# Layer 1 attention with a context: projections of the next two heads in three pieces, and three PSUM banks for transposes in that stage

## The chip, the cores and the metric

The kernel runs on one core of one Trainium2 chip, as one program. The metric is the device time of one execution in microseconds (us); the median of several runs stands for a version. A core has a matrix engine (TensorE, PE in the profile; its weight loads are listed as PEld), a vector engine (VectorE, DVE), a scalar engine (ScalarE, ACT), GpSimd (POOL) and SyncE (SP, which here issues DMAs). Each engine runs its own instructions in order and waits for others through semaphores. PE writes its results to PSUM, which this program uses as banks of 128 partitions by 512 float32; DVE and ACT carry ("evacuate") them from there to SBUF, from where PE takes its operands.

## The reference

A post-norm decoder of two layers over 8 batches of 512 tokens of width 256, with a context of 64 tokens for each batch, all in float32. Six steps follow one another, each with a residual and a layer norm:

```
x = LN(x + L0_attn(x))          # 16 heads of 16, scores times a decay of the distance
x = LN(x + L0_xattn(x, ctx))    # attention to the context
x = LN(x + L0_ffn(x))           # butterfly maps around a GELU
x = LN(x + L1_attn(x))          # 16 heads of 64, rotary, causal
x = LN(x + L1_xattn(x, ctx))    # the stage that is changed most
x = LN(x + L1_ffn(x))           # 8 experts, the best 2 for each token
```

What matters here is the fifth:

```
def _L1_xattn_ref(x1, x2, Wq1, Wk1, Wv1, Wk2, Wv2, Wo, bo):   # 8 heads of 64
    q1, k1, v1 = heads(x1 @ Wq1), heads(x1 @ Wk1), heads(x1 @ Wv1)
    k2, v2 = heads(x2 @ Wk2), heads(x2 @ Wv2)
    k, v = concat(k1, k2), concat(v1, v2)                     # 512 + 64 keys
    attn = softmax(q1 @ k.T * 64 ** -0.5)
    return (attn @ v) @ Wo + bo
```

The sixth, the experts, begins with a routing: a norm, a transposition, a product with the router's weights, the best two of eight, and for each token its rank in its expert's list, by which its row is scattered to memory.

## The kernel before, in words

Time order is batch by batch inside a stage, and stage by stage. In the profiled execution the stages lie about so: layer 0 self-attention 0 to 830 us, layer 0 context attention and feed-forward to 1262, layer 1 self-attention to 2234, layer 1 context attention to some 3130, the experts to 3660, and the last norm.

**PSUM.** Three pools are open at a time: `s` (tiles of two banks, for scores and wide products), `t` (one bank, tiles for transposes) and `o` (one bank, for outputs that are accumulated). Layer 0 self-attention has 3, 1 and 1 such tiles; everything after it 2, 2 and 2, which is eight banks. A pool gives its buffers in turn, and a tile waits until the buffer's earlier tile has been read. `evac` (L96 to L104) carries a bank to SBUF, on DVE and ACT in turns: L102 is DVE's copy, L104 ACT's.

**Layer 1 with the context** is a software pipeline (`_pipeline`, L32). Its units are (batch b, pair of heads c, block of 128 queries i), 8 by 4 by 4 = 128. In step n each stage runs on unit n minus its lag, in the order of the list; after the stages, one piece of postponed work (`put_off`) runs. The PE's order is exactly this program order (`manual_schedule`), while a scheduler places the instructions of DVE and ACT. The stages:

- `l1x_pre`, lag 0, works only at i = 0. At c = 0 it transposes the batch's x (`x_transposed`, L192) and makes the context's values (L1008) for this batch in 64 partitions, `vx`. Then for the pair of heads it makes q and k (L1020) in one `s` tile, evacuated by ACT (L1022, q) and DVE (L1023, k), and v (L1027) in a `t` tile, evacuated by ACT (L1035).
- `l1x_scores`, lag 1: for each of two heads j the scores with 512 keys (L1047) and with 64 context keys (L1048) in one `s` tile; DVE takes the maximum (L1049), ACT the exponential with its sum (L1050), and `scaled` (L883 to L885) divides on DVE.
- `l1x_transposes`, lag 3: eight 128x128 transposes (L287) in two `t` tiles named tP, each evacuated by `evac`.
- `l1x_values`, lag 7: the product with v (L1081), accumulated in an `o` tile over the four key blocks; at the fourth also the context's values (L1088), and `out_done` starts the output projection (L233, by postponed pieces).
- `l1x_last_transposes`, lag 3, stands last in the list: the transposes of the 64 context columns of both heads (L1069) in a third `t` tile tP2 of that step.

The postponed work of a finished batch is, a piece for every second step: the output projection in two pieces (L233), then `route_norm`, `route_transposes` (tiles tZ, L1146, evacuated by ACT to `xnT`, L1147), `route_picks` (tile o_r, L1161) and `route_places` (tile o_rank, L1200 to L1204; then on POOL the scatters L1216). `xnT` shares the tag "xT", which has two buffers, with the transposed x of `x_transposed`.

**Layer 0 self-attention** (L580 to L612) runs over 32 units of (batch, four heads). A unit has four steps kt. Each makes scores for the softmax (`l0_probs`), values (`l0_values`) and the maxima two units ahead (`l0_maxima`, L419); at kt = 3 a piece from the list `later` follows (the transposes and the output of a finished batch, whose norm ends with ACT's L215 on x, or the preparation of the next one). After the four steps comes `l0_project`, the q and k of three units ahead (L402, L403, evacuated by ACT at L404 and L405). Here a scheduler places PE's instructions too; around these lines the order it gives is the program's.

**Experts.** A pipeline over blocks of 256 or 128 token rows: load, transposes (tZ, L1351), up (s_h, L1373), down (o_y, L1390), and a scattered addition on POOL (L1411). The first block's rows are read back from `rows_in`, after the scatters.

Of the kernel before, what the change touches and what calls it, by code (L numbers as in the profile page):

```python
# [18 lines left out]
P = 128  # L19
# [30 lines left out]
def decoder_kernel(ctx: ExitStack, tc: tile.TileContext, a: dict, out: bass.AP):  # L50
# [19 lines left out]
    @contextmanager  # L70
    def psum(name, s, t, o):

        with (
            tc.tile_pool(name=f"ps_s{name}", bufs=s, space=PSUM) as pp["s"],
            tc.tile_pool(name=f"ps_t{name}", bufs=t, space=PSUM) as pp["t"],
            tc.tile_pool(name=f"ps_o{name}", bufs=o, space=PSUM) as pp["o"],
        ):
            yield

    def phase(name):  # L80
# [3 lines left out]
    def slot(name):  # L84
        return ring.tile([P, SLOT], F32, tag="slot", name=name)
# [6 lines left out]

    def o_tile(name):
        return pp["o"].tile([P, 512], F32, tag="o", name=name)

    n_evac = [0]  # L96

    def evac(dst, src):

        n_evac[0] += 1  # L100
        if n_evac[0] % 2:
            dve.tensor_copy(dst, src)  # L102
        else:
            act.copy(dst, src)  # L104
# [119 lines left out]
    def project_and_norm(b, lhs, w, n, plus, later=None):  # L224

        r = r_tile()

        def piece(i2):
            o = o_tile("o_out").rearrange("p (i n) -> p i n", i=2)
            for j in range(2):  # L230
                i = 2 * i2 + j
                for c in range(n):
                    pe.matmul(  # L233
                        o[:, j, :],
                        lhsT=lhs[:, c, i * P : (i + 1) * P],
                        rhs=w[:, c, :],
                        start=(c == 0),
                        stop=(c == n - 1),
                    )
# [303 lines left out]
    with tc.tile_pool(name="bfly", bufs=1, side="right") as bfly, phase("l0_self") as ph, psum("a", 3, 1, 1):  # L543
# [76 lines left out]
    ctx.enter_context(psum("b", 2, 2, 2))  # L620


    wqT = slot("wqT").rearrange("p (c n) -> p c n", c=KC)
# [347 lines left out]
        )  # L971


    q1_k1 = slot("q1_k1")
    v1_k2 = slot("v1_k2")
    v2_o = slot("v2_o")
# [10 lines left out]

    pts = [[slot("pt").rearrange("p (k n) -> p k n", k=NT) for _ in range(2)] for _ in range(2)]
    for c in range(4):
        o = o_tile("o_k2")  # L990
# [10 lines left out]
    def l1x_pre(b, c, i):  # L1001
        if i:
            return
        if c == 0:
            xT = x_transposed(b)
            o = o_tile("o_v2")
            for kc in range(KC):
                pe.matmul(  # L1008
                    o[0:S2, :], lhsT=ctxT[:, kc, b * S2 : (b + 1) * S2], rhs=wv2[:, kc, :], start=(kc == 0), stop=(kc == KC - 1)
                )  # L1010
            vx = work.tile([P, S], F32, tag="lat", name="vx")
            evac(vx[0:S2, :], o[0:S2, :])
            live["xT", b], live["vx", b] = xT, vx
        xT = live["xT", b]
        cols = slice(c * P, (c + 1) * P)
        q, k = qk_tiles()
        s = s_tile("s_qk")
        for j, w in enumerate((wq1, wk1)):
            for kc in range(KC):
                pe.matmul(s[:, j, :], lhsT=w[:, kc, cols], rhs=xT[:, kc, :], start=(kc == 0), stop=(kc == KC - 1))  # L1020

        act.mul(q, s[:, 0, :], 0.125)  # L1022
        dve.tensor_copy(k, s[:, 1, :])  # L1023
        t = t_tile("t_v")
        for j in range(NT):
            for kc in range(KC):
                pe.matmul(  # L1027
                    t[:, j, :],
                    lhsT=xT[:, kc, j * P : (j + 1) * P],
                    rhs=wv1[:, kc, cols],  # L1030
                    start=(kc == 0),
                    stop=(kc == KC - 1),
                )
        v = ph.tile([P, NT, P], F32, tag="vc", name="vc", bufs=3)
        act.copy(v, t)  # L1035
        live["qkv", b, c] = q, k, v

    def l1x_scores(b, c, i):
        q, k, _ = live["qkv", b, c]
        p = p_tile(S + S2, bufs=4)  # L1040
        sums = col("sums", 4)
        nm = col("nm", 2)
        for j in range(2):
            h = 64 * j
            lhsT = q[h : h + 64, i * P : (i + 1) * P]
            s = s_tile("s_sc").rearrange("p t n -> p (t n)")
            pe.matmul(s[:, 0:S], lhsT=lhsT, rhs=k[h : h + 64, :], start=True, stop=True)  # L1047
            pe.matmul(s[:, S : S + S2], lhsT=lhsT, rhs=k2[h : h + 64, c, b * S2 : (b + 1) * S2], start=True, stop=True)  # L1048
            dve.tensor_reduce(nm[:, j : j + 1], s[:, 0 : S + S2], AX.X, ALU.max, negate=True)  # L1049
            act.activation(  # L1050
                p[:, j, :], s[:, 0 : S + S2], AF.Exp, bias=nm[:, j : j + 1], accum_out=sums[:, j : j + 1]
            )
        scaled(p, sums, S + S2)
        live["p", b, c, i] = p

    def l1x_transposes(b, c, i):
        p = live["p", b, c, i]
        if i == 0:
            live["pt", b, c] = pts[c % 2], ph.tile([P, 2, S], F32, tag="pt2", name="pt2")
        pt, _ = live["pt", b, c]  # L1060
        probs_transposed(p, [pt[j][:, :, i * P : (i + 1) * P] for j in range(2)], NT)

    def l1x_last_transposes(b, c, i):

        p = live.pop(("p", b, c, i))
        _, pt2 = live["pt", b, c]
        t = t_tile("tP2")
        for j in range(2):
            pe.transpose(t[0:S2, j, :], p[:, j, S : S + S2], ident)  # L1069
        evac(pt2[0:S2, :, i * P : (i + 1) * P], t[0:S2, 0:2, :])  # L1070

    def l1x_values(b, c, k):

# [11 lines left out]
            return  # L1085
        for j in range(2):
            h = c * P + 64 * j
            pe.matmul(o[64 * j : 64 * (j + 1)], lhsT=vx[0:S2, h : h + 64], rhs=pt2[0:S2, j, :], start=False, stop=True)  # L1088

        def plus():  # L1090
            xb = work.tile([P, NT, D], F32, tag="att", name="xb")
# [63 lines left out]

    def route_picks(b):
        xnT = live.pop(("xnT", b))
        o = o_tile("o_r")[:, 0 : NT * NE].rearrange("p (i e) -> p i e", e=NE)
        for i in range(NT):
            for c in range(KC):  # L1160
                pe.matmul(  # L1161
# [33 lines left out]
    def route_places(b):  # L1195

        picks, both = live.pop(("picks", b))
        o = o_tile("o_rank")
# [184 lines left out]
    def moe_down(n):  # L1383
        _, mine, size = where[n]
        h = live.pop(("h", n))
        xr, _, w2, cells = live.pop(("load", n))
        o = o_tile("o_y").rearrange("p (i n) -> p i n", i=TILES)
        for i in range(size):
            for f in range(8):
                pe.matmul(  # L1390
# [159 lines left out]
```

## Time and profile before

| | us |
|---|---|
| three runs | 3712.23, 3716.97, 3719.49 |
| median | 3716.97 |
| the profiled execution | 3704.71 |
| its span, first to last instruction | 3703.0 |
| PE busy in the span | 3483.6 (94%) |
| DVE busy | 2190.3 (59%) |
| ACT busy | 1447.7 (39%) |
| POOL busy | 1091.5 (29%) |

The profile is one execution. A group of the profile is a source line, an engine, and what it writes and reads; its busy time is the sum over its instructions, and "idle before" is time in which the engine stood still just ahead of an instruction of that group, with the event that ended the wait. The timeline gives neighbouring instructions of one group as one row with a count. A float32 product appears as several records for one call: `x8` for q and k is two products in two parts each, and two records for every part. "PEclk" and the clock of a window are the share of the full TensorE clock that was granted.

### The profile page before, as it was taken

The page shows a single profiled execution, that of the slowest core. Times are in us where ns is not written, and L with a number is a line of the kernel's source. Part 1 is how long each engine was busy: PE and PEld are TensorE (multiplying, and loading weights), DVE is VectorE, ACT ScalarE, POOL GpSimd, SP SyncE. Part 2 cuts the span into 40 slices and gives each one's busy share as a digit, 9 for nine tenths or more (in the row PEclk, how much of TensorE's full clock was granted, in tenths as well). Part 3 has the DMA queues.
Part 4 walks back from the last instruction along what each step waited for, and adds up shares of the span by engine and source line. Part 5 has one row for each costly group of instructions (what it writes and reads, how often), then busy time and mean ns, then how long its engine had stood idle before and what let it go on. Part 6 is the DMA issues. An engine that isn't in the chain of part 4 may idle for free. (4 is left out here: it accounts for less than half of the span.)

```text
span 3703.0 us, 53042 instructions
## 1 busy us (share of the span) xinstructions
PE 3483.6 (94%) x19862; PEld 2149.2 (58%) x19862; DVE 2190.3 (59%) x6160; ACT 1447.7 (39%) x2949; POOL 1091.5 (29%) x960
## 2 busy tenths in 40 slices
PE   8999899988999899999999999999999998999995
PEld 3344334446666556665666665555555555888884
DVE  5766777647666377778777775665666655110102
ACT  2444444443333244445444443433334333222222
POOL 3877787751211122222222210010101101222222
PEclk8999999987999999999999999999999999999997
DMA  4100011120000395233222320000000001766674
GB/s 130 30 24 24 24 37 36 35 59 9 4 1 1 84 277 120 35 41 40 37 35 35 41 41 1 6 13 18 18 11 14 18 12 58 241 188 180 185 232 136
DMA packets 165363, 233.94 MB, mean 63 GB/s; under 512 B 26441, under 2 KB 128521, under 8 KB 165106
## 3 DMA queue, kind: packets, MB, share of 16 engines
q1 hardware_dynamic: 138370, 174.78, 15.1%
q0 software_dynamic: 25584, 51.57, 9.4%
q10 hardware_dynamic: 1152, 4.19, 0.3%
q8 instruction: 157, 2.57, 0.3%
q14 instruction: 100, 0.82, 0.1%
HBM read 135.83 MB, written 61.11 MB: 53 GB/s over the span
## 5 line engine op out<-in xcount | busy, mean ns | idle before, releaser
L424 DVE CUSTOM_DVE_ANT_0 scored<-s_sc,decay 128x512 f32<-128x512 f32 x512 | 323.2, 687 | 231.1 <-PE s_sc L419 229.9
L853 POOL DMA_DIRECT2D qk<-turned x256 | 202.8, 1206 | 668.8 <-PE t_v L860 284.1
L477 ACT ACTIVATE pt<-s_st 128x1024 f32<-128x1024 f32 x256 | 261.3, 1024 | 263.0 <-PE s_st L473 232.0
L277 ACT ACTIVATE p<-p,nm 128x128 f32<-128x128 f32 (+3 forms) x512 | 283.1, 554 | 160.4 <-DVE nm L275 157.5
L104 ACT COPY pt<-tP 128x512 f32<-128x512 f32 (+2 forms) x416 | 212.5, 511 | 298.3 <-PE tP L931 196.9
L1050 ACT ACTIVATE p<-s_sc,nm 128x576 f32<-128x576 f32 x256 | 189.7, 743 | 294.6 <-DVE nm L1049 256.5
L885 DVE TENSOR_SCALAR p<-p,rsum 128x576 f32<-128x576 f32 (+4 forms) x768 | 296.2, 427 | 5.5
L1410 DVE TENSOR_SCALAR y<-o_y,share 128x256 f32<-128x256 f32 x71 | 31.4, 480 | 403.6 <-PE o_y L1390 403.6
L1373 PE MATMUL s_h<-xnT,we 128*128 128x256 f32 (+1 forms) x1248 | 262.4, 364 | 1.9 <-DMA we<-in_mo_w 1.9
L102 DVE COPY pt<-tP 128x512 f32<-128x512 f32 (+2 forms) x416 | 248.3, 597 | 14.8 <-PE tP L1069 6.8
L1390 PE MATMUL o_y<-we,h 128*128 128x256 f32 x1136 | 251.6, 379 | 0.0
L265 DVE CUSTOM_DVE_ANT_0 p<-s_sc,tabs 128x128 f32<-128x128 f32 (+3 forms) x512 | 233.0, 484 | 20.7 <-PE s_sc L899 20.7
L1373 PEld LDWEIGHTS s_h<-xnT,we 128*128 128x128 f32 x1248 | 218.1, 193 | 27.1 <-DMA we<-in_mo_w 2.3
L1390 PEld LDWEIGHTS o_y<-we,h 128*128 128x128 f32 x1136 | 215.2, 190 | 28.9
L1411 POOL DMA_INDIRECT total<-y,to x71 | 110.1, 1551 | 397.3 <-DVE y L1410 206.0
L899 PE MATMUL s_sc<-qk 64*128 64x256 f32 (+3 forms) x1024 | 207.8, 477 | 18.3 <-DMA qk<-turned 16.3
L1049 DVE TENSOR_REDUCE nm<-s_sc 128x1 f32<-128x576 f32 x256 | 183.2, 749 | 57.2 <-PE s_sc L1048 56.7
L931 PEld LDWEIGHTS tP<-ident,p 128*128 128x128 f32 x1280 | 137.6, 141 | 127.2 <-issue 59.9
L931 PE MATMUL tP<-ident,p 128*128 128x128 f32 x1280 | 193.9, 284 | 12.0 <-DVE pt L102 8.0
L419 PE MATMUL s_sc<-k,q 32*128 32x512 f32 x1024 | 174.4, 680 | 28.4 <-ACT k L405 26.1
L1216 POOL DMA_INDIRECT rows_in<-z,irow x64 | 63.0, 985 | 451.9 <-DVE hit L1211 349.6
L955 PE MATMUL o_pv<-pt,vc 128*64 128x128 f32 (+1 forms) x2304 | 185.5, 294 | 0.0
(282 smaller groups left out, 6657.1 us busy)
## 6 DMA issues: line engine op xcount, KB each, us to landing
we<-in_mo_w SPq DMA_DIRECT2D x78, 1024.0 KB, 6.1
rows_in<-zero SPq DMA_DIRECT2D x64, 530.0 KB, 11.4
qk<-turned POOLq DMA_DIRECT2D x256, 128.0 KB, 4.5
coef<-in_ff_upw SPq DMA_DIRECT2D x40, 256.0 KB, 3.3
coef<-in_ff_dnw SPq DMA_DIRECT2D x40, 256.0 KB, 3.3
xr<-rows_in SPq DMA_DIRECT2D x32, 265.0 KB, 6.3
x<-in_x SPq DMA_DIRECT2D x8, 512.0 KB, 9.7
total<-x SPq DMA_DIRECT2D x8, 512.0 KB, 2.9
```

Of the source, the lines that this page charges most:

```text
L102: dve.tensor_copy(dst, src)
L104: act.copy(dst, src)
L265: dve.tensor_tensor_reduce(out=p[:, j, 0:n], in0=s[:, j, 0:n], in1=m, scale=1.0, scalar=-3.0e38, op0=op, op1=reduced, accum_out=mx[:, j : ...
L277: act.activation(p[:, j, 0:n], p[:, j, 0:n], AF.Exp, bias=nm[:, j : j + 1], scale=scale, accum_out=sums[:, at + j : at + j + 1],)
L424: dve.tensor_tensor_reduce(out=scored[:, h, :], in0=s[:, j, :], in1=decay[:, i, :], scale=1.0, scalar=-3.0e38, op0=ALU.mult, op1=ALU.max, ...
L477: act.activation(pt, s, AF.Exp, scale=1.0 / 16.0)
L853: pool.dma_start(out=qk[h : h + 32], in_=other[g : g + 32], accum_op=ALU.add)
L885: dve.tensor_scalar(p[:, j, 0:n], p[:, j, 0:n], rsum[:, j : j + 1], None, ALU.mult)
L899: pe.matmul(s[:, j, at : at + n], lhsT=q[h : h + 64, i * P : (i + 1) * P], rhs=k[h : h + 64, 0:n], start=True, stop=True,)
L931: pe.transpose(t[:, n, :], p[:, j, at * P : (at + 1) * P], ident)
L1373: pe.matmul(s[:, j, :], lhsT=w1[:, c, f * P : (f + 1) * P], rhs=xnT[:, c, :], start=(c == 0), stop=(c == KC - 1),)
L1390: pe.matmul(o[:, i, :], lhsT=h[:, f, i * P : (i + 1) * P], rhs=w2[:, f, :], start=(f == 0), stop=(f == 7),)
```

## The change

The PSUM pools are opened with waits for single tiles. Before the stage with the context, the pools 2, 2, 2 are closed and pools of 2 `s`, 3 `t` and 1 `o` opened, for this stage and the experts. With one `o` bank, everything except the accumulated o_pv takes a `t` tile (`u_tile`).

In the stage, the stages' lags become 0 (scores), 2 (transposes), 6 (values) and 0 (`l1x_ahead`, last). `l1x_pre` is split: the next pair of heads' q is made at i = 0, its k at i = 2, its v at i = 3, each in a `t` tile, behind the step's other work. At i = 1 the next batch's x is transposed (c = 2), or the context's values are made (c = 1, every second batch) for two batches in one product over 128 partitions; two DMAs make a second copy in which the halves are exchanged. The first batch's and heads' share is made ahead of the pipeline.

The second head's scores lie with the context columns ahead of the others, so that both heads' context columns are neighbours in `p`; one 128x128 transpose, ahead of the eight, takes the place of the two of 128x64. The context's values then use partitions 0 to 63 for one head and 64 to 127 for the other.

In layer 0 self-attention `l0_project` moves from the end of the unit to kt = 3, ahead of the postponed piece.

```diff
+        pool_of = partial(tc.tile_pool, space=PSUM, reuse_waits="tile")
         with (
...
+            pool_of(name=f"ps_s{name}", bufs=s) as pp["s"],
+            pool_of(name=f"ps_t{name}", bufs=t) as pp["t"],
+            pool_of(name=f"ps_o{name}", bufs=o) as pp["o"],
         ):
+            pp["one"] = o == 1
             yield
...
+    def u_tile(name):
+        return t_tile(name).rearrange("p i n -> p (i n)") if pp["one"] else o_tile(name)
...
-                elif later:
-                    later.pop(0)()
+                else:
+                    if kt and n + 3 < len(units):
+                        l0_project(*units[n + 3])
+                    if later:
+                        later.pop(0)()
                 for _ in range(3 - kt % 2):
                     next(butterfly, None)
-            if n + 3 < len(units):
-                l0_project(*units[n + 3])
...
+    banks.close()
+    ctx.enter_context(psum("c", 2, 3, 1))
...
+    def l1x_context_values(b):
+        o = u_tile("o_v2")
+        for kc in range(KC):
+            pe.matmul(o, lhsT=ctxT[:, kc, b * S2 : (b + 2) * S2], rhs=wv2[:, kc, :], start=(kc == 0), stop=(kc == KC - 1))
+        vx = [ph.tile([P, S], F32, tag=f"vx{n}", name="vx") for n in range(2)]
+        evac(vx[0], o)
+        for n in range(2):
+            sp.dma_start(out=vx[1][S2 * n : S2 * (n + 1)], in_=vx[0][S2 * (1 - n) : S2 * (2 - n)])
+        live["vx", b], live["vx", b + 1] = vx, vx[::-1]
+
+    def l1x_share(b):
+        live["xT", b] = x_transposed(b)
+
+    def l1x_project(b, c, what):
...
+            t = t_tile("t_qk").rearrange("p i n -> p (i n)")
...
+    def l1x_ahead(b, c, i):
+        nb, nc_ = (b, c + 1) if c < 3 else (b + 1, 0)
+        if i != 1:
+            if nb < NB:
+                l1x_project(nb, nc_, {0: 0, 2: 1, 3: 2}[i])
+        elif b + 1 < NB:
+            if c == 1 and b % 2:
+                l1x_context_values(b + 1)
+            elif c == 2:
+                l1x_share(b + 1)
...
+            pe.matmul(s[:, S * j : S * (j + 1)], lhsT=lhsT, rhs=k[h : h + 64, :], start=True, stop=True)
+            at = S - S2 * j
+            pe.matmul(s[:, at : at + S2], lhsT=lhsT, rhs=k2[h : h + 64, c, b * S2 : (b + 1) * S2], start=True, stop=True)
+            s = s[:, at * j : at * j + S + S2]
...
+        t = t_tile("tP2")[:, 0, :]
+        pe.transpose(t, p[:, S : S + P], ident)
+        evac(pt2[:, i * P : (i + 1) * P], t)
+        for j in range(2):
+            t = t_tile("tP")
+            for k in range(NT):
+                pe.transpose(t[:, k, :], p[:, (S + P) * j + k * P : (S + P) * j + (k + 1) * P], ident)
+            evac(pt[j][:, :, i * P : (i + 1) * P], t)
...
-            pe.matmul(o[64 * j : 64 * (j + 1)], lhsT=vx[0:S2, h : h + 64], rhs=pt2[0:S2, j, :], start=False, stop=True)
+            half = slice(64 * j, 64 * (j + 1))
+            pe.matmul(o[half], lhsT=vx[j][half, h : h + 64], rhs=pt2[half, :], start=False, stop=True)
...
     with phase("l1_context") as ph, tc.manual_schedule(engines={PE}):
+        l1x_share(0)
+        l1x_context_values(0)
+        for what in range(3):
+            l1x_project(0, 0, what)
         _pipeline(
             [(b, c, i) for b in range(NB) for c in range(4) for i in range(NT)],
-            [(0, l1x_pre), (1, l1x_scores), (3, l1x_transposes), (7, l1x_values), (3, l1x_last_transposes)],
+            [(0, l1x_scores), (2, l1x_transposes), (6, l1x_values), (0, l1x_ahead)],
             put_off,
         )
```

In `l1_context` o_k2, o_out, o_r and o_rank, and in the experts o_y, are asked for with `u_tile`.

More of the change, by code (lines that the diff above doesn't have):

```diff
@@ L71, in psum @@
     def psum(name, s, t, o):
+        pool_of = partial(tc.tile_pool, space=PSUM, reuse_waits="tile")
         with (
-            tc.tile_pool(name=f"ps_s{name}", bufs=s, space=PSUM) as pp["s"],
-            tc.tile_pool(name=f"ps_t{name}", bufs=t, space=PSUM) as pp["t"],
-            tc.tile_pool(name=f"ps_o{name}", bufs=o, space=PSUM) as pp["o"],
+            pool_of(name=f"ps_s{name}", bufs=s) as pp["s"],
+            pool_of(name=f"ps_t{name}", bufs=t) as pp["t"],
+            pool_of(name=f"ps_o{name}", bufs=o) as pp["o"],
         ):
+            pp["one"] = o == 1
             yield
@@ L228, in piece @@
         def piece(i2):
-            o = o_tile("o_out").rearrange("p (i n) -> p i n", i=2)
+            o = u_tile("o_out").rearrange("p (i n) -> p i n", i=2)
             for j in range(2):
@@ L618, in decoder_kernel @@
         dve.tensor_tensor(upb, o[:, 0:8], upb, ALU.add)
-    ctx.enter_context(psum("b", 2, 2, 2))
+    banks = ExitStack()
+    banks.enter_context(psum("b", 2, 2, 2))
     wqT = slot("wqT").rearrange("p (c n) -> p c n", c=KC)
@@ L989, in decoder_kernel @@
     for c in range(4):
-        o = o_tile("o_k2")
+        o = u_tile("o_k2")
         for kc in range(KC):
@@ L999, in decoder_kernel @@
         evac(k2[:, c, 0:NC2], o[:, 0:NC2])
[L1001 to L1013, printed above, removed]
+    def l1x_context_values(b):
[10 more added lines that the diff above has]
+    def l1x_project(b, c, what):
         xT = live["xT", b]
         cols = slice(c * P, (c + 1) * P)
-        q, k = qk_tiles()
-        s = s_tile("s_qk")
-        for j, w in enumerate((wq1, wk1)):
+        if what == 0:
+            live["qk", b, c] = qk_tiles()
+        if what < 2:
+            t = t_tile("t_qk").rearrange("p i n -> p (i n)")
             for kc in range(KC):
-                pe.matmul(s[:, j, :], lhsT=w[:, kc, cols], rhs=xT[:, kc, :], start=(kc == 0), stop=(kc == KC - 1))
-        act.mul(q, s[:, 0, :], 0.125)
-        dve.tensor_copy(k, s[:, 1, :])
+                pe.matmul(t, lhsT=(wq1, wk1)[what][:, kc, cols], rhs=xT[:, kc, :], start=(kc == 0), stop=(kc == KC - 1))
+            if what == 0:
+                act.mul(live["qk", b, c][0], t, 0.125)
+            else:
+                dve.tensor_copy(live["qk", b, c][1], t)
+            return
         t = t_tile("t_v")
@@ L1035, in l1x_pre @@
         act.copy(v, t)
-        live["qkv", b, c] = q, k, v
+        live["qkv", b, c] = *live.pop(("qk", b, c)), v
+    def l1x_ahead(b, c, i):
[8 more added lines that the diff above has]
+                l1x_share(b + 1)
     def l1x_scores(b, c, i):
@@ L1046, in l1x_scores @@
             s = s_tile("s_sc").rearrange("p t n -> p (t n)")
[L1047 to L1052, printed above, removed]
+            pe.matmul(s[:, S * j : S * (j + 1)], lhsT=lhsT, rhs=k[h : h + 64, :], start=True, stop=True)
+            at = S - S2 * j
+            pe.matmul(s[:, at : at + S2], lhsT=lhsT, rhs=k2[h : h + 64, c, b * S2 : (b + 1) * S2], start=True, stop=True)
+            s = s[:, at * j : at * j + S + S2]
+            dve.tensor_reduce(nm[:, j : j + 1], s, AX.X, ALU.max, negate=True)
+            act.activation(p[:, j, :], s, AF.Exp, bias=nm[:, j : j + 1], accum_out=sums[:, j : j + 1])
         scaled(p, sums, S + S2)
@@ L1056, in l1x_transposes @@
     def l1x_transposes(b, c, i):
-        p = live["p", b, c, i]
+        p = live.pop(("p", b, c, i)).rearrange("p j n -> p (j n)")
         if i == 0:
[L1059 to L1067, printed above, removed]
+            live["pt", b, c] = pts[c % 2], ph.tile([P, S], F32, tag="pt2", name="pt2")
+        pt, pt2 = live["pt", b, c]
+        t = t_tile("tP2")[:, 0, :]
+        pe.transpose(t, p[:, S : S + P], ident)
+        evac(pt2[:, i * P : (i + 1) * P], t)
         for j in range(2):
-            pe.transpose(t[0:S2, j, :], p[:, j, S : S + S2], ident)
-        evac(pt2[0:S2, :, i * P : (i + 1) * P], t[0:S2, 0:2, :])
+            t = t_tile("tP")
+            for k in range(NT):
+                pe.transpose(t[:, k, :], p[:, (S + P) * j + k * P : (S + P) * j + (k + 1) * P], ident)
+            evac(pt[j][:, :, i * P : (i + 1) * P], t)
     def l1x_values(b, c, k):
@@ L1157, in route_picks @@
         xnT = live.pop(("xnT", b))
-        o = o_tile("o_r")[:, 0 : NT * NE].rearrange("p (i e) -> p i e", e=NE)
+        o = u_tile("o_r")[:, 0 : NT * NE].rearrange("p (i e) -> p i e", e=NE)
         for i in range(NT):
@@ L1197, in route_places @@
         picks, both = live.pop(("picks", b))
-        o = o_tile("o_rank")
+        o = u_tile("o_rank")
         for i in range(NT):
@@ L1386, in moe_down @@
         xr, _, w2, cells = live.pop(("load", n))
-        o = o_tile("o_y").rearrange("p (i n) -> p i n", i=TILES)
+        o = u_tile("o_y").rearrange("p (i n) -> p i n", i=TILES)
         for i in range(size):
```

## The prediction

> **What bounds the kernel now.** I read the page's head first, then the windows by stage, then the waits of the stage that the change rewrites, then its timeline. Page and windows (us, then busy time of PE, PEld, DVE, ACT, POOL, the granted TensorE clock, DMA share, GB/s):
>
> ```profile
> span 3703.0 us, 53042 instructions
> ...
> PEclk8999999987999999999999999999999999999997
> ```
>
> ```profile
> 1262.00:2234.00 972.00, 940.55 (x6149) 591.55 (x6148) 743.40 (x2552) 450.69 (x1328) 217.83 (x273) 0.99 0.41 75
> 2234.00:3125.00 891.00, 837.09 (x4388) 485.27 (x4386) 550.27 (x1319) 345.11 (x816) 80.68 (x73) 0.96 0.04 13
> ```
>
> PE bounds both stages. In the second, layer 1 with the context (the one changed), it is idle for 54 of 891 us, and its clock is 0.96 where the stage before has 0.99. Which waits, in PE's weight loads there (total us, times, longest):
>
> ```profile
> PEld tP L1069 <- ACT pt L104: 71.6, 61, 2.4
> ...
> PEld tP L1069 <- DVE pt L102: 45.2, 38, 3.3
> ```
>
> The two small context transposes L1069 are the third tile of a step for two t banks, so they wait for an evacuation. PE's timeline around a change of heads (start, us, engine, line; idle before in brackets):
>
> ```profile
> 2593.83 0.41 PE L1069 MATMUL tP<-ident,p 128*64 128x128 f32 x2 [0.48 <-ACT pt L104]
> 2594.07 3.62 PE L233 MATMUL o_out<-v_o,aT 128*128 128x256 f32 x16
> 2597.53 3.60 PE L1020 MATMUL s_qk<-xT,q_k 128*128 128x512 f32 x8
> 2600.96 1.95 PE L1027 MATMUL t_v<-v_k,xT 128*128 128x128 f32 x16
> 2602.84 1.12 PE L1047 MATMUL s_sc<-k,q 64*128 64x512 f32 x2
> ...
> 2605.18 1.12 PE L1047 MATMUL s_sc<-k,q 64*128 64x512 f32 x2 [1.05 <-DVE k L1023]
> ...
> 2606.40 1.09 PE L287 MATMUL tP<-ident,p 128*128 128x128 f32 x8
> 2607.43 1.08 PE L1081 MATMUL o_pv<-pt,vc 128*64 128x512 f32 x4
> 2610.05 0.41 PE L1069 MATMUL tP<-ident,p 128*64 128x128 f32 x2 [1.55 <-ACT pt L104]
> 2610.39 1.52 PE L1047 MATMUL s_sc<-k,q 64*128 64x512 f32 x4
> ...
> 2618.24 1.08 PE L1081 MATMUL o_pv<-pt,vc 128*64 128x512 f32 x4
> 2619.25 1.08 PE L1088 MATMUL o_pv<-pt,vx 64*64 64x512 f32 x4
> 2620.26 0.41 PE L1069 MATMUL tP<-ident,p 128*64 128x128 f32 x2
> 2620.59 1.14 PE L1047 MATMUL s_sc<-k,q 64*128 64x512 f32 x4
> ```
>
> Three things are to be seen. A block's cost is the distance to the next start where nothing waits: q and k projection 3.43, v 1.88, values 1.01, context values 1.01, a piece of output 3.46. The first scores of a head wait 1.05 for the k just made. After the 1.55 us stall the scores take 1.52 instead of 1.14: the clock has dropped.
>
> **The stage's floor and excess.** From the first x transpose (2232.5) to the end of the last output piece (3132.4) it is 900 us. Undisturbed blocks (lower quartile of start-to-start distances) times their number: scores 1.23x128=157.4, eight transposes 1.02x128=130.6, L1069 0.25x128=32, values 129.3, context values 32.3, projections 5.31x32=170, x transposes 9.6, context v (L1008) 2.38x8=19, output 3.46x16=55.4, routing (tZ 1.22, picks 1.78, ranks 3.2, seven each) 43.4. Sum 779, so 121 us are excess: some 36 clock ((1-0.96)x891), some 85 waits (29 idle directly before L1069, 39 by which value blocks with such a wait in them exceed 1.01, the rest k at head changes, ranks waiting for DVE, and the filling of the pipeline).
>
> **The change, part by part.**
> *Work.* The two L1069 transposes become one 128x128: -32+128x0.128 (1.02/8) = -15.6. Context v for two batches at once: four times about 1.85 instead of eight times 2.38, -11.6. New floor 752, a gain of **27**. The second head's scores lie mirrored in their two banks, so that the context columns meet: the same lengths, nothing. The evacuation count stays, its shape goes from 64x256 (DVE 409 ns, ACT 361) to 128x128; put at the same. The eight DMAs that swap the halves of vx (two 128 KB on SP per pair; nearest row qk<-turned, 128 KB, 4.5 us to landing) are needed over 45 us later; behind them on SP stand only the residual stores. Nothing.
>
> *Waits removed.* In pieces, q, k and v of the next head are done a step or more before its first scores: six waits of 1.05 go. With three t banks a plain step takes four tiles (tP2, tP, tP, piece), each on the bank of the tile three before, some 4 us earlier on PE; laid out with exp 743+199, maximum 749, scale 518 and evacuations of 681 (DVE) and 579 (ACT), the banks are free at 3.3 to 4.8 us after a step's scores, steps being 4.4 to 5.3 us long on PE. So L1069's wait goes. Late next: the ranks (7.0 us over six waits), which the change doesn't touch, and the score banks, still two.
>
> *A wait added.* The tag xT has two buffers, for xT and for the routing's xnT. xT(b+1) is now made in step (b,2,1), so xnT(b-1), one step later, must overwrite xT(b), still read by the v piece of (b,2,3). ACT's evacuation to xnT waits for that piece; both tZ banks are held; tP2, tP, tP and t_v all pass through the third. Six times, 2.6 to 3.5 us of waiting for evacuations in turn, and about 1.7 of low clock: 6x4.7 = **28**, ends 10 and 35. Behind the waiting instruction on ACT are the next exps.
>
> *Excess after:* 28, filling 6, draining 6, ranks, late DVE and score banks 19, clock 8: **67**. The stage 752+67 = 819 against 900: gain **81**.
>
> *Clock rule.* Some 20 stretches at 0.5, 75 us together, begin within 5 us of a PE gap, and these gaps last 0.5 to 1.9 us. The Trainium skill (TensorE: Matmul & The Clock Gate, "Why this matters for your kernels") warns of gaps over about 3 us. By the rule the 36 us are not of these stalls and stay: gain 81-28 = 53. By the row they go with the gaps; I take the row, keeping 8 of the 36 (besides the ten above), and 53 within the range.
>
> *A rule against the change.* Context values now use row halves 0-63 and 64-127, both into one o bank; before, both used rows 0-63 (1.01 the pair). The skill (TensorEngine Tiling (Array Packing), "Gotcha 1: PSUM Pressure") says that different row tiles can't access one PSUM bank at a time. No row shows this case. Nearest, L1088: nothing lost. If the pair ran in series: four records at 0.43 (3.43/8) = 1.72, +0.71x32 = 23. I take 0, since they write different partitions; 23 stays in the range.
>
> *Experts.* The first expert waits for a chain from the last early ranks: first scatter 3.9 us later, eight scatters of about 2.75, row load, then
>
> ```profile
> 3136.80 0.44 PE L1351 MATMUL tZ<-ident,xr 128*128 128x128 f32 x2 [4.43 <-DMA xr<-rows_in]
> 3140.45 6.56 PE L1373 MATMUL s_h<-xnT,we 128*128 128x256 f32 x20 [1.87 <-DMA we<-in_mo_w]
> ```
>
> 29.3 us after the ranks' end (3107.5). PE now fills 24.8 of them; with shorter lags only 21 to 23: +**3** (0 to 8). o_y and tZ sharing three banks instead of two and two: 0 (±2), PE being busy 527 of 535 us there.
>
> *Layer 0.* l0_project moves ahead of the postponed piece. At six changes of batch PE stands still because ACT, in order, normalises x (waiting 8.70 us for DVE) before q, k and exp:
>
> ```profile
> 451.18 2.07 ACT L215 ACTIVATE x<-r,ve,rs 128x256 f32<-128x256 f32 x4 [8.70 <-DVE ve L212]
> ...
> 454.36 2.98 PE L419 MATMUL s_sc<-k,q 32*128 32x512 f32 x8 [4.78 <-ACT k L405]
> ```
>
> q and k now pass the normalisation, but exp doesn't: 0.9 to 1.5 us of the 4.8 go, six times, 5 to 9. Against it, q/k projections come directly behind scores and wait 0.1 to 0.2 for a score bank, some 23 times: 3, and 1 for the piece's later evacuation. Net gain **3**, ends -6 and +25 (all six gaps and their low clock). POOL's order is unchanged there. Stages two and three keep their order; the pools' waits for single tiles find none there that would end later: 0.
>
> **Sum.** -81+3-3 = **-81**: 3704.7, the profiled execution, to 3624; it is 12 under the median of the runs, 3717, so **3636** there.
>
> **Rivals.**
> *All excess goes* but 25 (filling, ranks): stage 777, gain 123, **3594**. For: l1_self runs at 0.99 with this engine mix. Against: the xT wait. 0.13.
> *Most is given back.* DVE is 62% busy (550 of 891) and gets 67% of a shorter stage; evacuations stand behind 749 ns maxima and the one-bank steps spread to neighbours: excess 110, gain 38, **3679**. 0.14.
> *Slower: three banks for everything.* Tiles, pieces, routing and output now share three where four (t and o) served. If an evacuation is late in every step by t, the stage is 752+128t+20; it decides from t = 1.0 (880+20=900). At 1.3, twice the 0.68 evacuation standing in line, it is 938: **3755**. Against: the 4 us between uses of a bank. 0.05.
> *The change doesn't do what it says:* the projections moved but PE's floor and clock remain, within 7 us of before: 0.03.
>
> **Numbers.** Forecast (gain 45 to 110) 0.65. The range, 3594 to 3690, holds it, half of the first rival and most of the second. 0.2% of the time, 7.4 us, is what can be told from no change: faster 0.91, same 0.03, slower 0.06.
>
> **What would show it.** Context stage near 819 us at a clock of 0.98 or more; tP2 without a wait on pt in plain steps, but six waits around (b,2,2) with t_v and tP behind one another; no wait of scores for k; experts' first tZ some 3 us more idle; layer 0 gaps near 3.5 us. It is wrong if the clock stays at 0.96, if context values take over 1.5 us a pair, or if tP waits in every step.

## The result, and the profile after

| | before | after |
|---|---|---|
| median of the runs, us | 3714.6 (4 runs, 3707.37 to 3719.49) | 3652.66 (4 runs, 3650.17 to 3667.75) |
| the profiled execution, us | 3704.71 | 3650.17 |
| layer 1 with the context, first x transpose to last output piece, us | 899.8 | 860.6 |
| of it at a granted clock of 0.5, us | 75.1 in 17 stretches | 71.7 in 14 |
| from there to the first expert's product, us | 8.1 | 11.7 |

The ratio is 0.9848, with a 95% interval of 0.982 to 0.9875: the kernel became 1.5% faster, some 56 us, where 81 had been forecast. The page's head of the kernel after, and its window over the changed stage (us, busy time of PE, PEld, DVE, ACT, POOL, granted clock, DMA share, GB/s):

```profile
span 3648.5 us, 52874 instructions
```

```profile
2213.16:3073.76 860.60, 804.25 (x4285) 471.57 (x4283) 536.93 (x1323) 337.82 (x816) 81.50 (x74) 0.96 0.05 15
```

Between the same marks of before the row was:

```profile
2232.53:3132.37 899.84, 845.93 (x4429) 492.27 (x4427) 552.62 (x1325) 346.68 (x818) 83.44 (x76) 0.96 0.04 13
```

PE's busy time there is 42 us less, and the stage is 39 us shorter. The idle time has not shrunk: 56 us of 861, where it was 54 of 900, at the same clock of 0.96. Where it stands now, in the waits of PE's weight loads in that stage (total us, times, longest):

```profile
PEld t_qk L1034 <- ACT pt L110: 38.6, 39, 1.8
...
PEld tP L1097 <- DVE k L1039: 26.8, 6, 5.8
```

and in the groups of PE (busy us, mean ns, idle just before and what ended it):

```profile
L1097 PE MATMUL tP<-ident,p 128*128 128x128 f32 x1024 | 145.5, 285 | 40.6 <-DVE k L1039 25.4 <-DVE pt L108 7.3 <-ACT pt L110 6.0
L1034 PE MATMUL t_qk<-xT,q_k 128*128 128x512 f32 x256 | 126.6, 618 | 9.5 <-ACT pt L110 5.3 <-DVE pt L108 3.3
...
L1117 PE MATMUL o_pv<-pt,vx 64*64 64x512 f32 x128 | 34.4, 614 | 0.0
```

The long line of waits for pt in front of the small transposes is gone, and those of t_qk, which look large as waits of weight loads, cost PE only 9.5 us. But 40.6 us of idle time stand in front of the eight transposes, 25.4 of them for one event: DVE's evacuation of k, six times, 2.6 to 5.6 us each. The context values take 614 ns each, as before.

What holds that evacuation back is seen in the timeline of all engines around the first of the six (start, us, engine, line; idle before):

```profile
2416.27 1.98 PE L1034 MATMUL t_qk<-xT,q_k 128*128 128x512 f32 x4
...
2419.42 0.33 PE L1092 MATMUL tP<-ident,p 128*128 128x128 f32 x1
2419.59 0.60 PE L1097 MATMUL tP<-ident,p 128*128 128x128 f32 x4
2420.96 0.96 POOL L1245 DMA_INDIRECT rows_in<-z,irow  x1 [1.82 <-DMA rows_in<-z,irow]
2423.53 0.17 DVE L1221 COPY z<-tokens_at 128x4 f32<-128x4 f32 x1 [5.45 <-DMA rows_in<-z,irow]
2423.61 0.68 DVE L1039 COPY k<-t_qk 128x512 f32<-128x512 f32 x1
...
2424.35 1.11 PE L1097 MATMUL tP<-ident,p 128*128 128x128 f32 x4 [4.16 <-DVE k L1039]
```

The routing's rows `z` have one buffer. DVE's copy of the token numbers into it (170 ns, for the next batch) needs nothing but that buffer, so the scheduler had put it far ahead of the rest of its batch's routing, where the eight scatters of the batch before, one after the other on POOL, still read `z`. DVE waits 5.45 us for the last of them; k, next in its queue, holds a transpose bank; the second tP of the step needs that bank. In the kernel before the same copy waited less (DVE's waits there, then after):

```profile
DVE z L1192 <- DMA rows_in<-z,irow: 13.9, 6, 2.8
```

```profile
DVE z L1221 <- DMA rows_in<-z,irow: 32.8, 6, 6.9
```

The other stall is the one forecast, in step (b,2,2):

```profile
2368.39 1.04 PE L1175 MATMUL tZ<-ident,z 128*128 128x128 f32 x8
...
2370.59 0.33 PE L1092 MATMUL tP<-ident,p 128*128 128x128 f32 x1
...
2372.02 0.28 DVE L108 COPY pt<-tP 128x128 f32<-128x128 f32 x1
...
2372.36 0.66 PE L1097 MATMUL tP<-ident,p 128*128 128x128 f32 x4 [1.44 <-DVE pt L108]
...
2373.05 0.59 ACT L110 COPY pt<-tP 128x512 f32<-128x512 f32 x1
...
2373.69 0.66 PE L1097 MATMUL tP<-ident,p 128*128 128x128 f32 x4 [0.68 <-ACT pt L110]
```

Both tZ banks are held, so the three transposes of the step go through one bank, each behind the evacuation of the one before.

### The profile page after: what moved, and what is told of

The parts are those of the page before. It is cut to its first block, busy times and chain, and to the rows that moved or that the text cites. A ratio compares the mean times of both kernels' runs of the same rounds, so it can differ in the third digit from the quotient of the medians.

```text
span 3648.5 us, 52874 instructions
## 1 busy us (share of the span) xinstructions
PE 3429.4 (94%) x19718; PEld 2117.7 (58%) x19718; DVE 2173.6 (60%) x6158; ACT 1437.9 (39%) x2947; POOL 1092.5 (30%) x960
## 5 line engine op out<-in xcount | busy, mean ns | idle before, releaser
L108 DVE COPY pt<-tP 128x512 f32<-128x512 f32 (+2 forms) x416 | 235.9, 576 | 8.0 <-PE tP L1097 3.6
L907 PE MATMUL s_sc<-qk 64*128 64x128 f32 (+3 forms) x1024 | 205.8, 474 | 14.3 <-DMA qk<-turned 12.7
L425 PE MATMUL s_sc<-k,q 32*128 32x512 f32 x1024 | 174.5, 671 | 25.8 <-ACT pt L483 23.2
```

The costliest lines, as they stand in the source:

```text
L907: pe.matmul(s[:, j, at : at + n], lhsT=q[h : h + 64, i * P : (i + 1) * P], rhs=k[h : h + 64, 0:n], start=True, stop=True,)
```

## The experiments

Times are medians; ratios are against the kernel before, run on the same chip. "Stage" is layer 1 with the context, from its first x transpose to its last output piece, in the run's own profile. It is the sharper measure: the stages ahead of it ended anywhere from 2206 to 2233 us in the traces of the kernels that keep layer 0 as the change has it, though PE's order in them is the same. In e7 the first x transposes come ahead of the context's keys, and its stage is counted from the context's values.

| run | us | ratio, interval | stage, us | of it at clock 0.5, us |
|---|---|---|---|---|
| the change | 3652.66 | 0.9848 [0.982, 0.9875] | 860.6 | 71.7 |
| e1_token_order | 3625.45 | 0.9756 [0.974, 0.9772] | 818.2 | 30.7 |
| e2_xnT_own_buffer | 3633.01 | 0.978 [0.9762, 0.9799] | 836.6 | 58.0 |
| e3_both | 3601.25 | 0.9694 [0.9679, 0.9709] | 798.4 | 27.3 |
| e4_layer0_undone | 3656.39 | 0.9851 [0.9829, 0.9874] | 856.2 | 64.9 |
| e5_before_tile_waits | 3707.31 | 0.9987 [0.9976, 0.9998] | 903.8 | 85.3 |
| e6_before_banks_231 | 3702.32 | 0.9964 [0.9951, 0.9978] | 897.3 | 88.7 |
| e7_both_banks_222 | 3762.9 | 1.0138 [1.012, 1.0155] | 962.5 | 61.4 |
| e8_layer0_norm_later | 3586.46 | 0.9655 [0.964, 0.9671] | 800.3 | 30.7 |
| e9_pieces_at_once | 3650.05 | 0.9847 [0.9827, 0.9868] | 851.2 | 81.9 |
| e10_before_token_order | 3697.49 | 0.9959 [0.9943, 0.9975] | 890.8 | 71.7 |
| e11_layer0_norm_earlier | 3551.89 | 0.9577 [0.9557, 0.9598] | 800.1 | 30.7 |
| e12_ranks_earlier | 3545.44 | 0.9547 [0.9533, 0.9561] | 796.2 | 20.5 |

### The two waits

```diff
-        dve.tensor_copy(z[:, :, D + NE], tokens_at[:, b * NT : (b + 1) * NT])
+        tc.keep_in_program_order(dve.tensor_copy(z[:, :, D + NE], tokens_at[:, b * NT : (b + 1) * NT]))
```

> The change, with the routing's copy of the token numbers (z<-tokens_at on DVE) kept at its place in the program instead of half a step of routing earlier. Theory A (that copy waits for the scatters of the batch before, and the evacuation of k behind it holds a transpose bank): the six PE gaps of 2.6 to 5.6 us before tP (25.4 us) go, and the half clock that follows four or five of them (some 30 us at 0.5, 15 us of work) with them: 35 to 40 us faster than the change, about 3613. Rival B (the three transpose banks are the limit, and the copy only happens to be named): another evacuation is late in its place, less than 10 us. Rival C (low clock comes of the many small stalls, not of these gaps): the clock of the stage stays at 0.96 and about 25 us are gained.

Measured: 27 us faster than the change by the medians, the stage 42.4 us shorter, and 41 us less of it at half clock. In the stage the order of PE and POOL is the same, on ACT one evacuation at the stage's end has changed places, and on DVE only this copy has moved. So the copy was the cause (theory A). Of the 42.4 us, 25.3 are idle time of PE, and 17.1 are busy time with the same instructions, of which 41 us less at half clock explain up to 20.5. The group of the eight transposes in e1:

```profile
L1097 PE MATMUL tP<-ident,p 128*128 128x128 f32 x1024 | 141.5, 281 | 15.2 <-DVE pt L108 7.3 <-ACT pt L110 6.0 <-DVE xT L108 1.6
```

Rival B falls, since no other evacuation took the place of k; C falls too, since the clock of the stage is 0.98.

```diff
-        xnT = work.tile([P, KC, S], F32, tag="xT", name="xnT")
+        xnT = [work.tile([P, S], F32, tag="lat", name="xnT") for _ in range(KC)]
```

> The change, with the routing's transposed rows xnT in the two half-size buffers that the context values used before, so that they share nothing with the transposed x. Prediction's step: the one-bank steps cost 28 us, so 28 faster. By the trace of the change they show 1.44+0.68 us of idle PE six times (12.7 us) and about 20 us at half clock behind them: 20 to 23 faster, about 3631. Rival (the bank is late anyway, by the evacuations' queue): under 8. The DVE copy's six gaps stay.

Measured: 20 us faster, the stage 24.0 shorter. The forecast's 28 was near, and a little high; the 20 to 23 read from the trace of the change were nearer.

> Both edits. If A and the one-bank step are two separate costs they add up: 55 to 63 us faster than the change, about 3593, stage with the context near 800 us at a clock of 0.98 or more. If one only hides the other (rival B): no more than the larger of the two.

Measured: 51 us faster, the stage 62.2 shorter, against 42.4+24.0 = 66.4 for the two apart: they add up. Its window over the stage, and the group of the eight transposes:

```profile
2228.33:3026.76 798.43, 781.12 (x4285) 461.14 (x4283) 537.03 (x1324) 337.70 (x816) 82.16 (x75) 0.98 0.05 16
```

```profile
L1097 PE MATMUL tP<-ident,p 128*128 128x128 f32 x1024 | 139.0, 280 | 1.6 <-DVE xT L108 1.6
```

40.6 us of idle time have become 1.6, and the clock is 0.98. PE's busy time fell by 23 us with the same instructions, since fewer of them ran at half clock.

e10 makes the edit of e1 in the kernel before.

> The kernel before with the copy of the token numbers kept at its place. If the wait of that copy cost the kernel before as it costs the change: 10 or more faster, as it is 13.9 us on DVE there (6 of 2.0 to 2.8). If the change brought it onto the path: within 5 of 3714, because the earlier, looser order gave DVE time to catch up.

Measured: 0.41% (0.25 to 0.57) faster, some 15 us, and the stage 9 to 13 shorter than in the two traces with the order of before (899.8 and 903.8). The first expectation holds: the copy had cost the kernel before some ten us already, and the change made forty of it.

### The banks and the pieces

The prediction gave the wait of the small transposes to the third transpose bank. Three runs take bank and pieces apart. First, before with the banks alone:

```diff
+    banks.close()
+    ctx.enter_context(psum("c", 2, 3, 1))
...
-            o = o_tile("o_v2")
+            o = u_tile("o_v2")
```

(and `u_tile` likewise for the other outputs)

> The kernel before with the banks of the change alone in the context stage and the experts (2 score tiles, 3 transpose banks, 1 output bank; the other outputs take a transpose bank); its pipeline, its projections in one and its two small transposes stay. Prediction's reading: the wait of the small transposes for a bank (29 us of idle PE before them, 39 in stretched value blocks, and most of 36 of clock) is the third bank's to take away, the wait for k at six heads stays: 45 to 65 faster, context stage 835 to 855. Rival: the evacuations are late whatever the banks; the gain is that of the pieces and the saved work (27), and the banks alone give under 15.

Measured: 0.36% (0.22 to 0.49) faster, the stage 897.3. The rival's bound was right. The longest wait of its weight loads for another engine, and two groups of PE:

```profile
PEld tP L1077 <- ACT p L1058: 41.1, 46, 1.6
```

```profile
L1055 PE MATMUL s_sc<-k,q 64*128 64x512 f32 x510 | 185.8, 660 | 11.2 <-DVE k L1031 6.3 <-ACT p L1058 4.9
...
L1028 PE MATMUL s_qk<-xT,q_k 128*128 128x512 f32 x248 | 116.1, 612 | 8.4 <-ACT p L1058 8.4
```

No wait for an evacuation (pt) leads any more, and PE's idle time directly before the small transposes has fallen from 29 us to 3. But the time has only moved. From start to start, eight transposes and values take 273 us where they took 315 in the kernel before, and small transposes and scores take 275 where they took 242; 14 us more are at half clock. With the bank free, PE is through a step sooner and comes to the scores sooner, and now waits for ACT's exponential. PE itself stands only 13.3 us for it (4.9 and 8.4 in the groups above), so most of the 41 us of the weight loads cost PE no idle time; that the rest of the lost time is the score bank which exp still reads is a reading of the trace, not a test. (e6 has not the waits for single tiles; they did nothing with the banks of before, in e5 below, and were not tried with these banks and without the pieces.) Then the version of e3 with the banks of before:

```diff
-    ctx.enter_context(psum("c", 2, 3, 1))
+    ctx.enter_context(psum("c", 2, 2, 2))
```

> The version with both waits taken away (3601), with two transpose banks and two output banks instead of three and one; four transpose tiles of a step take turns on two banks. If the third bank carries the gain: each step loses some 0.3 to 0.7 us waiting for an evacuation and more clock, 40 to 90 slower than 3601. If the pieces carry it: under 15 slower, as their places between scores and transposes give the evacuations time.

Measured: 162 us slower than e3 (stage 962.5 against 798.4), and slower than the kernel before. It is far beyond both expectations:

```profile
L1097 PE MATMUL tP<-ident,p 128*128 128x128 f32 x984 | 159.3, 287 | 137.0 <-ACT pt L110 82.3 <-DVE pt L108 54.7
```

137 us of idle time stand before the tP alone, 1.1 us a step: with four tiles a step on two banks a tile takes the bank of the one but last, whose evacuation is still under way. Last, e3 with q, k and v one after the other:

```diff
-        if i != 1:
+        if i == 3:
             if nb < NB:
-                l1x_project(nb, nc_, {0: 0, 2: 1, 3: 2}[i])
-        elif b + 1 < NB:
+                for what in range(3):
+                    l1x_project(nb, nc_, what)
+        elif i == 1 and b + 1 < NB:
```

> The version with both waits taken away (3601, context stage 798), its banks, its joined transpose and its lags, but with q, k and v of the next heads made one after the other at i = 3 instead of at i = 0, 2 and 3. Theory D (the pieces make the steps even: a step without one is 3.4 us on PE, while scores, maxima and exponentials need 4.15 us until a score bank is free): three steps of four wait about 0.7 us for a score bank, 96x0.7 = 67 us, and more low clock, less what the long step gives back: 40 to 80 slower, with waits of the scores for ACT's exp. Rival (the gain is the third bank and the saved work): under 12 slower.

Measured: 49 us slower than e3, the stage 52.8 longer, 54.6 us more of it at half clock. A step without a piece in its timeline:

```profile
2574.71 1.08 PE L1110 MATMUL o_pv<-pt,vc 128*64 128x512 f32 x4
...
2576.60 0.74 ACT L1083 ACTIVATE p<-s_sc,nm 128x576 f32<-128x576 f32 x1 [2.40 <-DVE nm L1082]
...
2577.49 1.12 PE L1078 MATMUL s_sc<-k,q 64*128 64x512 f32 x2 [1.70 <-ACT p L1083]
...
2578.69 1.84 PE L1078 MATMUL s_sc<-k,q 64*128 64x512 f32 x2
2580.33 0.53 PE L1080 MATMUL s_sc<-k,q 64*128 64x64 f32 x2
```

The next scores wait 1.70 us for the exponential of this step's first scores, and the second pair of them takes 1.84 us where the first took 1.12: the clock has dropped. Theory D is what the runs show, though with less idle time than it was given (25.8 us in gaps of over 0.2 us, against 16.1 in e3) and more clock (up to 27 us, half of 54.6); the remaining 15 us or so are blocks, of scores above all, that take longer while PE counts as busy. So bank and pieces work only together. The bank without the pieces wins 2.5 to 6.4 us of stage against the kernel before; the pieces without the bank lose 63 against it (164 against e3); and with the bank, piling the pieces up loses 53 against e3.

### Layer 0 and the other edits

e4 puts `l0_project` back behind the postponed piece.

> The change without the move in layer 0 (projections again at the end of the unit, behind the postponed piece). Prediction: net 3 us, so 3 slower than the change, within noise; the gaps of PE at the changes of batch in layer 0 go back from what the change shows to 4.8 us. Rival: the 19 us by which the context stage starts earlier in the trace of the change come of this move: then 15 to 19 slower, and the context stage starts at about 2232 again.

Measured: 3656.39 against 3652.66, with overlapping intervals. PE's gaps at the six changes of batch are 4.1 to 4.8 us there and 3.85 to 3.9 in the change, 25.6 against 23.2 us in sum. The move brings 2.4 us in the trace, which the time can't tell from nothing. The context stage does start late again in e4's trace, at 2235.6 us, as the rival had it, but so it does in e1's (2240.3), which has the move: the start follows the half clock ahead of it, as the end of the next section shows, and not the move.

e5 is the kernel before with `reuse_waits="tile"` for the PSUM pools.

> The kernel before with nothing but the PSUM pools' waits for single tiles. Prediction: none of these waits ends later or earlier, so 3715 within noise, and a context stage of 900 us. Rival: the stage of the change is 39 to 44 us shorter by the traces and the time 62, so 15 to 20 us come of something else that the change touches everywhere: then 3695 to 3700.

Measured: 0.13% (0.02 to 0.24) faster, some 5 us, stage 903.8. The rival falls; no 15 us come from there.

In the change, layer 0's remaining gap ends with ACT:

```profile
451.43 1.08 ACT L221 ACTIVATE x<-r,ve,rs 128x256 f32<-128x256 f32 x2
452.41 1.91 ACT L483 ACTIVATE pt<-s_st 128x1024 f32<-128x1024 f32 x2
```

```profile
453.47 1.55 PE L425 MATMUL s_sc<-k,q 32*128 32x512 f32 x4 [3.85 <-ACT pt L483]
```

exp (pt) stands behind the norm's application to x. e8 and e11 build on e3 and put that application off, its instructions kept in program order:

```diff
+            def shift():
+                x = dve.scalar_tensor_tensor(ve, mv[:, :, 0], -1.0, rs, ALU.mult, ALU.mult)
...
+            def apply():
+                for i in range(NT):
+                    x = act.activation(dst[:, i, :], r[:, i, :], AF.Identity, bias=ve[:, i : i + 1], scale=rs[:, i : i + 1])
...
+                if kt == 0 and applied:
+                    applied.pop(0)()
```

In e8 both run at kt = 1 of the next unit; in e11, which the diff shows, `shift` runs at kt = 0 and `apply` at kt = 1.

> The version with both waits taken away, and in layer 0 the application of the norm to x (one on DVE, four on ACT) put off from the batch's last piece to the second step of the next unit, behind that unit's first exponentials. By the trace of the change PE stands 3.85 to 3.9 us six times at the change of batch until ACT's exp behind these four has run (23 us), with 6.8 us at half clock behind each (20 us of work): 25 to 43 faster than 3601, if exp was what came last. Rival: DVE's maxima, with the statistics of the norm in the queue ahead of them, are late next: under 12.

Measured: 15 us faster than e3, between the two expectations. The gaps only moved by a step and shrank to 3.02 us: ACT's norm stood waiting for DVE's shift, which was issued with it, and exp behind both.

> As the version with the norm of layer 0 put off (3586), where PE still stands 3.0 us six times because ACT's norm waits for DVE's shift, behind the maxima; here the shift is issued one step before ACT's four. If that is the whole wait: the six gaps of 3.0 us go (18 us) and some half clock, 15 to 30 faster than 3586. If DVE itself is what is late: under 6.

Measured: 35 us faster than e8, more than the 15 to 30 expected of the six gaps alone. None of the six is left, and layer 0 spends 34 us at half clock instead of 82 in e3.

e12 drops one empty piece ahead of the last early batch's `route_norm`.

> As the run before, and the routing of the last batch but one starts one step of postponed work sooner, so that its ranks come some 5 us earlier against the end of the stage. The wait of the first expert behind the stage's end (about 10 us in these versions) falls by 4 to 6: 3 to 6 faster than the run before. If the chain isn't the scatters' but the expert's weights': no change.

Measured: 6 us faster than e11, the upper end of what was expected. The first expert's transpose waits 3.05 us for its rows, where it waited 8.70 in e11 and 9.00 in the change (e12, then the change):

```profile
2979.04 0.69 PE L1399 MATMUL tZ<-ident,xr 128*128 128x128 f32 x2 [3.05 <-DMA xr<-rows_in]
```

```profile
3082.76 0.69 PE L1380 MATMUL tZ<-ident,xr 128*128 128x128 f32 x2 [9.00 <-DMA xr<-rows_in]
```

e12 is the fastest of all, 4.5% (4.39 to 4.67) under the kernel before and 107 us under the change by the medians.

## Why the prediction was right, and where it was not

**Direction, range and likeliest case: right, the last in part by luck.** 3652.66 lies between 3594 and 3690; the gain was 62 by the medians and 56 by the ratio, where 81 was forecast. But in the profiled executions the stage gained 39 us (43 against e5's trace), which is under the 45 where the likeliest case begins. Some 20 us more came ahead of the stage, where the forecast had put 3.

**The signs it had named.** Two of the three signs of being wrong stayed away: context values take 1.01 us a pair, and the small transposes don't wait in every step. The third came: the stage's clock stayed at 0.96. The stage took 861 us where 819 was the sign of being right.

**The saved work: right, but for the cost of the pieces.** With the prediction's method (lower quartiles of start-to-start distances times their number) the blocks of the change add up to some 757 us, against 752 in the sum and 779 before. The joined transposes save 17.6 us (15.6 forecast) and the context values about 11 (11.6). What the sum put at nothing is that q, k and v cost more in pieces: 1.82, 1.82 and 1.98 us, together 5.62 where it kept 5.31, so 10 us over 32 pairs of heads; other blocks came out some 5 us shorter.

**The wait added, six one-bank steps at 28: right, slightly large.** 24.0 us of stage in e2, 20 between e1 and e3.

**The step that failed: "ranks, late DVE and score banks 19, clock 8".** Among the waits that would be "late next" the prediction named the ranks and the score banks. It missed the copy of the token numbers, whose wait for the scatters stood in the profile of before with 13.9 us, as a wait of DVE that looked harmless (e10 shows that it wasn't quite). With k on a transpose bank it came onto PE's path and cost 42.4 us of stage (e1), idle time and clock together. So the excess, forecast at 67 us, is some 104 (860.6 less 757). Without the copy the stage is 818.2 us; the forecast, which didn't have it, was 819. That they meet so closely is chance, as the pieces' cost and the slightly large 28 cancel in part. What I should have done: for each instruction in front of the moved k evacuation on DVE, ask what it waits for.

**What removes the wait of L1069: right on the wait, wrong on what it brings.** "With three t banks [...] So L1069's wait goes": with the bank alone it does go (29 us of idle time to 3 in e6), but the time comes back at the scores, and the stage gains 2.5 to 6.4 us. The gain needs bank and pieces together (e6, e7, e9). What the pieces do besides was not in the prediction at all: they lengthen the short steps, and in e9, where they are not spread, the scores wait for exp.

**Rules against rows.** Clock: in the kernel before, 75.1 us in 17 stretches are at half clock though no gap of PE in the stage is over 2.4 us, so the warning of gaps over about 3 us (the Trainium skill, TensorE: Matmul & The Clock Gate, "Why this matters for your kernels") doesn't cover this stage. By the prediction's reading the 36 us should go with the short gaps. In the change they stayed (71.7 us at half clock) with other gaps in their place, and in e3, where these are gone, the half clock is down to 27.3 us. So far the reading holds, and the forecast of which gaps would remain failed. But it is no measure: e6 has 19 us less idle time than before and 14 us more at half clock, and e7, with 146 us idle between its marks, has only 61.4. Row halves into one bank (TensorEngine Tiling (Array Packing), "Gotcha 1: PSUM Pressure"): 614 ns for one before and after, and 1.01 us a pair at the median; the 23 us that the rule would cost do not occur here.

**Experts, +3:** 8.1 became 11.7 us in the two traces, but this wait lies between 8.1 and 11.6 in the traces with before's pipeline and between 7.8 and 12.3 in those with the change's (e12, which moves the ranks, has 6.1), so 3 can't be told from the spread. **Layer 0, +3:** 2.4 in the gaps.

**Rivals.** "All excess goes" (3594) is near e3: that was there to be had, and two waits kept it. "Most is given back" had nearly the stage's numbers, an excess of 110 and a gain of 38 where 104 and 39 were measured, but not its reason: 42.4 us hang on one copy (e1), and the trace shows no general lateness of evacuations. The slower case, three banks for everything, didn't come: late evacuations in every step are seen only where there are two banks (e7).

**Open.** The stage explains 39 to 43 us of a gain whose interval is 46 to 67. In the two profiled executions the rest lies ahead of the stage, which starts 19.4 us earlier in the change, and it is clock: 129.7 us at half clock up to there, where it was 167.3, and half of the difference is 18.8. This half clock varies as much between traces of kernels with the same order of PE there (180.9 us in e1, 150.2 in e3). Neither the tile waits (e5) nor the move in layer 0 (e4) is seen to bring it; whether the change has a part in it is not shown.

## What to carry to other kernels

When a piece of work gets a place in a scarce bank, its evacuation's queue becomes part of the critical path: look through what stands ahead of it on that engine, above all for small copies that need only a buffer and that a scheduler has put far ahead. In this pipeline of unequal steps, even steps and a third bank paid only together: without the bank evacuations came late, without even steps the softmax did. Read a harmless-looking wait of a side engine as a price that the next change may have to pay.

## What the runs showed of the hardware

Half clock adds to what a stall costs: taking away six gaps of 25.4 us in sum (e1) took away 41 us at a clock of 0.5, and 17.1 us of busy time with it. Stretches at half clock also follow short gaps: in e3 one begins 4.7 us after a gap of 0.56 us, with none longer in the 12 us before. The sum of the gaps does not set them: PE is idle for 35 us of the stage in e6 and for 146 in e7, with 88.7 and 61.4 us at half clock. What starts a stretch stays open.
